# Two graph layers on degree-sorted nodes: edge j of a node as row j of its own partition, summed by VectorE, and experts that scatter their rows to the output

## The chip, the cores and the metric

The kernel runs on one core of one Trainium2 chip. The metric is the device time of one execution in microseconds, given as the median of several runs. A core has TensorE (PE, with its weight loads shown apart as PEld), VectorE (DVE), ScalarE (ACT), GpSimd (POOL) and SyncE (SP). SP, ACT and POOL issue the transfers of this kernel; an indirect transfer, which takes the address of each row from a column of indices, is issued by POOL.

## The reference

There are 6250 nodes with 256 features, and 100000 directed edges `src -> dst`, sorted by `dst`, with 64 features each. Four residual stages follow one another, each on a layer norm (LN) of x:

```python
ft = (feat @ W_fc).reshape(N, 8, 32)                 # graph layer 0
e  = leaky_relu(eh[src] + ee + et[dst])              # eh, et: ft with attn_h, attn_t; ee: edge_attr with attn_e
a  = softmax of e over the edges of each dst
x += segment_sum(ft[src] * a, dst) + bias
x += shared_mlp(LN(x)) + the best 2 of 4 experts, mixed by their gates    # FFN 0
feat_src = LN(x) @ W_src                             # graph layer 1
r  = segment_sum(feat_src[src], dst) / max(deg, 1) + LN(x)
x += relu(batch_norm(r) * gamma + beta)
x += relu(relu(LN(x) @ W1[i] + b1[i]) @ W2[i] + b2[i])   # i: the best of 32 experts of each node
```

Everything is float32.

## The kernel before

**Tiles.** The nodes lie in their given order in 49 tiles of 128 (one node on a partition, 106 in the last). The node table x stays on the chip (`x_all`, 128 x 49 x 256).

**Prep.** SP loads x, a tile at a time (L216). POOL's queue fills two tables in DRAM with zeros (L221, L226). `edge_ranges` (L150 and on) finds where the edges of each tile begin: it loads `dst` on 125 partitions (L155), and takes minima, maxima and comparisons on 128 x 49 x 50 values (among them the reduce at L185). `node_tile` (L258) normalizes a tile, transposes it (L264), multiplies by the weights (L269), and stores rows of 264 floats, features and eight `eh`, into the DRAM table `tab0`. `edge_block` (L281) loads 2048 edges' attributes through ACT's queue (L285), transposes them (L289), copies them (`evacuate`, L121 and L123), multiplies (L295) and stores eight logits an edge to `ee_d`. A maximum over all nodes and edges (L322 to L324) shifts the exponents. Two loops over further windows of edges (L424) run no round on this input.

**Graph layer 0.** A tile takes one window of 128 x 18 = 2304 consecutive edges, from the first edge of the tile on; edge p·18+k lies on partition p. An edge's partition says nothing of its destination. For each tile, in an order written out by hand under `manual_schedule`:
- `gather` (L772): 18 indirect transfers on POOL, each of 128 rows of `tab0`, into one of 8 buffers of 6 columns.
- `turn` (L779, L781): ACT makes the transposed one-hot matrix of destinations from a copy of `dst` spread over all partitions (`load_row`).
- `look_up` (L792): PE multiplies it by `et`, so each edge finds its destination's term.
- `one_hots` (L801): DVE makes the upright one-hot.
- `weights` (L812 to L821): DVE adds the logits, leaky ReLU, ACT takes the exponential.
- `spread` (L826): DVE multiplies the gathered rows by the weights, 6 columns of 256 at a time.
- `sums` (L832): PE adds the rows of each node, 18 products of one-hot and rows accumulated in PSUM (`pa`). They release the buffers to later gathers.
- `join` (L837 to L844): divides by the sum of the weights and adds to x.

FFN 0 is a generator (`ffn0`, by groups of 4 tiles, 24 steps a group); `advance` deals its steps among the parts of a tile, six a tile. The rest runs after the last tile. Its last steps store LN(x) @ W_src as rows of the DRAM table `tab1`.

**Graph layer 1.** The same windows: 18 gathers of `tab1` a tile (L358), a one-hot on DVE (L370), 18 products on PE (L414), a copy by ACT (L933).

**Rest.** Batch norm: LN again, mean and square sums by products with ones, two passes over 49 tiles (L971 to L985). `route` (L1019 and on), by groups of 4: normalize, add to x, LN, 32 router logits, the best expert, and the node's rank in it. 49 row scatters on POOL sort the LN rows by expert into `xs_d` (L1101). 80 rounds, each of 128 slots of one expert: load, transposes (L1116), two products (L1121, L1127), ReLU, store to `ys_d` by SP. Then 49 gathers of `ys_d` by each node's slot (L1135), the addition of x (L1137) and the store. Reciprocal square roots are ACT's Ln and Exp (L95, L96), each with the load of a function table.

Of the kernel before, what the change touches and what calls it, by code (L numbers as in the profile page):

```python
# [23 lines left out]
SLOPE = 0.2  # L24

K = 18
W = P * K

SPREAD = 60.0

S = 6
NG = 8

G = 4


@with_exitstack
def tile_gnn_ffn(ctx: ExitStack, tc: tile.TileContext, a: dict, out: bass.AP):
# [10 lines left out]
    ACC = D + HEADS + 1  # L49
    GROUPS = [range(g, min(g + G, NT)) for g in range(0, NT, G)]  # L50
    rows = lambda t: P if t < NT - 1 else LAST

# [4 lines left out]
    tab0 = dram.tile([N, D + HEADS], F32, name="tab0")  # L57
    tab1 = dram.tile([N, D], F32, name="tab1")
    ee_d = dram.tile([E, HEADS], F32, name="ee_d")
    xs_d = dram.tile([NS * P, D], F32, name="xs_d")  # L60
    ys_d = dram.tile([NS * P, D], F32, name="ys_d")

    dst_f = dram.tile([E], F32, name="dst_f")

    more_d = dram.tile([NT * P, ACC], F32, name="more_d")

    x = const.tile([P, NT, D], F32, name="x_all")
    et_m = const.tile([P, NT, 2 * HEADS], F32, name="et_m")
    shift_q = const.tile([P, NT, HEADS], F32, name="shift_q")
    rdeg = const.tile([P, NT], F32, name="rdeg")  # L70
    mv_all = const.tile([P, NT, 2], F32, name="mv_all")
    rs_all = const.tile([P, NT], F32, name="rs_all")

    ident = const.tile([P, P], F32, name="ident")
    make_identity(nc, ident)
    ones = const.tile([P, P], F32, name="ones")
    nc.gpsimd.memset(ones, 1.0)
    iota = const.tile([P, P], F32, name="iota")
    nc.gpsimd.iota(iota, pattern=[[1, P]], base=0, channel_multiplier=0,
                   allow_small_or_imprecise_dtypes=True)  # L80
    zeros = const.tile([P, 512], F32, name="zeros")
    nc.vector.memset(zeros, 0.0)
# [6 lines left out]
    def rsqrt(pool, out_ap, var_ap, n, eps):  # L89

        v = pool.tile([P, n], F32, name="rsq_v")
        r = pool.tile([P, n], F32, name="rsq_r")
        u = pool.tile([P, n], F32, name="rsq_u")
        nc.vector.tensor_scalar(v, var_ap, eps, None, op0=ALU.add)
        nc.scalar.activation(r, v, AF.Ln)  # L95
        nc.scalar.activation(r, r, AF.Exp, scale=-0.5)  # L96
        nc.vector.tensor_mul(u, r, r)
        nc.vector.tensor_mul(u, u, v)
        nc.vector.tensor_scalar(u, u, -0.5, 1.5, op0=ALU.mult, op1=ALU.add)
        nc.vector.tensor_mul(out_ap, r, u)  # L100

    def ln_stats(pool, tiles):

        t0, n = tiles[0], len(tiles)
        st = pool.tile([P, G, 6], F32, name="ln_st")
        for i, t in enumerate(tiles):
            nc.vector.bn_stats(st[:, i, :], x[:, t, :])
            nc.vector.bn_aggr(mv_all[:, t, :], st[:, i, :])
        rsqrt(pool, rs_all[:, t0:t0 + n], mv_all[:, t0:t0 + n, 1], n, LN_EPS)

    def ln_apply(out_ap, t):
        nc.vector.tensor_scalar(out_ap, x[:, t, :], mv_all[:, t, 0:1], rs_all[:, t:t + 1],  # L112
                                op0=ALU.subtract, op1=ALU.mult)
# [11 lines left out]
    def max_over_partitions(pool, psum, vals, n):  # L125

        p1 = psum.tile([P, P], F32, name="mx_p")
        nc.tensor.transpose(p1[:n, :], vals, ident)
        m = pool.tile([P, 1], F32, name="mx_m")
        nc.vector.tensor_reduce(m[:n], p1[:n, :], axis=AX.X, op=ALU.max)  # L130
        p2 = psum.tile([P, P], F32, name="mx_p")
        nc.tensor.transpose(p2[:, :n], m[:n].to_broadcast([n, P]), ident[:n, :n])
        r = pool.tile([P, n], F32, name="mx_r")
        nc.vector.tensor_copy(r, p2[:, :n])
        return r


    lo_b = const.tile([P, NT], F32, name="lo_b")
    start_i = const.tile([1, NT], I32, name="start_i")
    more_i = const.tile([1, NT], I32, name="more_i")  # L140
    wins_i = const.tile([1, NT], I32, name="wins_i")
    gate_i = const.tile([1, 2], I32, name="gate_i")
    t128 = const.tile([P, NT], F32, name="t128")
    nc.gpsimd.iota(t128, pattern=[[P, NT]], base=0, channel_multiplier=0,
                   allow_small_or_imprecise_dtypes=True)

    def edge_ranges(pool, psum):

        NP_ = 125
        J = E // NP_  # L150
        S = 16
        NG = J // S
        assert NP_ * NG * S == E
        d = pool.tile([P, J], I32, name="er_d", bufs=1)
        nc.scalar.dma_start(d[:NP_], dst.rearrange("(p j) -> p j", p=NP_))  # L155
        as_f = pool.tile([P, J], F32, name="er_df", bufs=1)
        nc.vector.tensor_copy(as_f[:NP_], d[:NP_])
        nc.scalar.dma_start(dst_f.rearrange("(p j) -> p j", p=NP_), as_f[:NP_])
        mn = pool.tile([P, NG], F32, name="er_mn", bufs=1)
        mx = pool.tile([P, NG], F32, name="er_mx", bufs=1)  # L160
        nc.vector.memset(mn, 1e9)
        nc.vector.memset(mx, -1.0)
        dv = d[:NP_].rearrange("p (g s) -> p g s", s=S)
        nc.vector.tensor_reduce(mn[:NP_], dv, axis=AX.X, op=ALU.min)
        nc.vector.tensor_reduce(mx[:NP_], dv, axis=AX.X, op=ALU.max)
        first = pool.tile([P, NG], F32, name="er_f", bufs=1)
        nc.gpsimd.iota(first, pattern=[[S, NG]], base=0, channel_multiplier=J,
                       allow_small_or_imprecise_dtypes=True)
        left = pool.tile([P, NG], F32, name="er_l", bufs=1)
        nc.vector.tensor_scalar(left, first, -1.0, float(E), op0=ALU.mult, op1=ALU.add)  # L170
        end = pool.tile([P, NG], F32, name="er_e", bufs=1)
        nc.vector.tensor_scalar(end, first, float(S), None, op0=ALU.add)
        tend = pool.tile([P, NT], F32, name="er_te", bufs=1)
        nc.vector.tensor_scalar(tend, t128, float(P - 1), None, op0=ALU.add)
        shp = [P, NT, NG]
        per_t = lambda v: v[:, :, None].to_broadcast(shp)
        per_g = lambda v: v[:, None, :].to_broadcast(shp)
        i1 = pool.tile(shp, F32, name="er_i1", bufs=1)
        i2 = pool.tile(shp, F32, name="er_i2", bufs=1)
        nc.vector.tensor_tensor(i1, per_g(mn), per_t(tend), op=ALU.is_le)  # L180
        nc.vector.tensor_tensor(i2, per_g(mx), per_t(t128), op=ALU.is_ge)
        nc.vector.tensor_mul(i1, i1, i2)
        res = pool.tile([P, 2 * NT], F32, name="er_res", bufs=1)
        nc.vector.tensor_mul(i2, i1, per_g(left))
        nc.vector.tensor_reduce(res[:, :NT], i2, axis=AX.X, op=ALU.max)  # L185
        nc.vector.tensor_mul(i2, i1, per_g(end))
        nc.vector.tensor_reduce(res[:, NT:], i2, axis=AX.X, op=ALU.max)
        r = max_over_partitions(pool, psum, res, 2 * NT)
        nc.vector.tensor_scalar(lo_b, r[:, :NT], -1.0, float(E), op0=ALU.mult, op1=ALU.add)
        nc.vector.tensor_scalar(start_i, lo_b[0:1], float(E - W), None, op0=ALU.min)  # L190

        span = pool.tile([1, NT], F32, name="er_sp", bufs=1)
        nc.vector.tensor_sub(span, r[0:1, NT:], lo_b[0:1])
        M = -(-E // W)
        steps = pool.tile([1, M], F32, name="er_st", bufs=1)
        nc.gpsimd.iota(steps, pattern=[[W, M]], base=W, channel_multiplier=0,
                       allow_small_or_imprecise_dtypes=True)
        cmp = pool.tile([1, NT, M], F32, name="er_c", bufs=1)
        nc.vector.tensor_tensor(cmp, steps[:, None, :].to_broadcast([1, NT, M]),
                                span[:, :, None].to_broadcast([1, NT, M]), op=ALU.is_lt)  # L200
        more = pool.tile([1, NT], F32, name="er_m", bufs=1)
        nc.vector.tensor_reduce(more, cmp, axis=AX.X, op=ALU.add)
        nc.vector.tensor_copy(more_i, more)
        nc.vector.tensor_scalar(wins_i, more, 1.0, None, op0=ALU.add)
        any_ = pool.tile([1, 1], F32, name="er_a", bufs=1)
        nc.vector.tensor_reduce(any_, more, axis=AX.X, op=ALU.max)
        nc.vector.tensor_scalar(gate_i[:, 0:1], any_, 1.0, float(NT), op0=ALU.min, op1=ALU.mult)

    with ExitStack() as st:
        pool = st.enter_context(tc.tile_pool(name="proj", bufs=3))  # L210
        one = st.enter_context(tc.tile_pool(name="proj1", bufs=1))
        psum = st.enter_context(tc.tile_pool(name="proj_ps", bufs=1, space=PSUM))

        nc.vector.memset(x[:, NT - 1, :], 0.0)
        for t in range(NT):
            nc.sync.dma_start(x[:rows(t), t, :], x_in[t * P:t * P + rows(t), :])  # L216


# [95 lines left out]
        for c in range(nb, NC_):  # L314
            edge_block(c)
# [852 lines left out]
```

## Time and profile before

| | us |
|---|---|
| median of 9 runs | 3951.92 (3931.8 to 3976.82) |
| the profiled execution | 3934.73 |
| its span | 3933.0 |
| first gather of layer 0 (L772) | 341.6 |
| first gather of layer 1 (L358) | 2149.8 |
| first scatter by expert (L1101) | 3663.1 |
| first gather of the experts' rows (L1135) | 3855.1 |
| mean granted clock of TensorE | 0.699 of full speed |

The profile is one execution, taken by the hardware profiler. A group's row gives the line in the kernel, the engine, the operation, `out<-in` and how often; behind the first bar the busy microseconds and the mean nanoseconds of one; behind the second the idle time of the engine just before such instructions and what ended most of it (`<-PE pa L832`: TensorE finishing its write of `pa` on line 832; `issue`: nothing that the profile shows). A row "by source" gives minimum, median and maximum duration and the first and last start. A row of a window gives its bounds and length, then busy time and count of PE, PEld, DVE, ACT and POOL, the granted clock, the DMA engines' busy share, and GB/s. A row of the timeline gives start, duration, and in brackets the idle time before.

### The profile page before, as it was taken

The page shows a single profiled execution, that of the slowest core. Times are in us where ns is not written, and L with a number is a line of the kernel's source. Part 1 is how long each engine was busy: PE and PEld are TensorE (multiplying, and loading weights), DVE is VectorE, ACT ScalarE, POOL GpSimd, SP SyncE. Part 2 cuts the span into 40 slices and gives each one's busy share as a digit, 9 for nine tenths or more (in the row PEclk, how much of TensorE's full clock was granted, in tenths as well). Part 3 has the DMA queues.
Part 4 walks back from the last instruction along what each step waited for, and adds up shares of the span by engine and source line. Part 5 has one row for each costly group of instructions (what it writes and reads, how often), then busy time and mean ns, then how long its engine had stood idle before and what let it go on. Part 6 is the DMA issues. An engine that isn't in the chain of part 4 may idle for free. (4 is left out here: it accounts for less than half of the span.)

```text
span 3933.0 us, 32320 instructions
## 1 busy us (share of the span) xinstructions
PE 2628.1 (67%) x9687; PEld 1800.1 (46%) x9688; DVE 1287.0 (33%) x3094; ACT 900.0 (23%) x1444; POOL 1883.1 (48%) x2087
## 2 busy tenths in 40 slices
PE   3993577866867776775786766667566666756191
PEld 3893555655555555554563333333333323445161
DVE  3551444443444443443352010010111001466153
ACT  1331333443344343343333000000000000032040
POOL 1124554544544454544421666666666666311415
PEclk9696667777777787777787566565666556765595
DMA  9354443433434343433310333333333333400255
GB/s 317 110 171 126 135 125 114 121 103 113 117 118 120 94 133 107 121 111 95 119 52 22 96 90 96 92 94 96 90 96 91 96 92 94 98 1 0 73 181 157
DMA packets 219168, 420.53 MB, mean 107 GB/s; under 512 B 70836, under 2 KB 142591, under 8 KB 212711
## 3 DMA queue, kind: packets, MB, share of 16 engines
q0 software_dynamic: 94000, 264.88, 22.7%
q1 hardware_dynamic: 100512, 113.49, 9.7%
q10 hardware_dynamic: 24472, 39.99, 3.6%
q8 instruction: 81, 1.33, 0.1%
q14 instruction: 103, 0.84, 0.1%
HBM read 361.16 MB, written 57.02 MB: 106 GB/s over the span
## 5 line engine op out<-in xcount | busy, mean ns | idle before, releaser
L772 POOL DMA_INDIRECT g<-tab,ix x882 | 837.6, 950 | 831.7 <-PE pa L832 535.6
L414 PE MATMUL pb<-g,oh 128*128 128x256 f32 x1764 | 823.1, 580 | 432.1 <-issue 310.5
L358 POOL DMA_INDIRECT g<-tab,ix x882 | 837.5, 950 | 408.8 <-issue 249.2
L414 PEld LDWEIGHTS pb<-g,oh 128*128 128x128 f32 x1764 | 408.5, 266 | 846.7 <-DMA g<-tab,ix 412.0
L832 PE MATMUL pa<-g,oh 128*128 128x265 f32 x1764 | 497.2, 438 | 16.4 <-DVE g L826 13.1
L370 DVE TENSOR_TENSOR oh<-iota_ps,df 128x2304 f32<-128x2304 f32 x49 | 125.3, 2558 | 1091.3 <-PE pb L414 586.9
L792 PE MATMUL pz<-et_m,oht 128*128 128x16 f32 x1764 | 295.0, 294 | 249.9 <-issue 212.0
L792 PEld LDWEIGHTS pz<-et_m,oht 128*128 128x128 f32 x1764 | 306.1, 250 | 293.7 <-issue 286.1
L832 PEld LDWEIGHTS pa<-g,oh 128*128 128x128 f32 x1764 | 372.8, 217 | 126.6 <-DVE g L826 27.1
L933 ACT COPY acc_all<-pb 128x256 f32<-128x256 f32 x49 | 18.2, 372 | 1237.1 <-PE pb L414 687.0
L779 ACT ACTIVATE oht<-db,nid 128x768 f32<-128x768 f32 x147 | 253.3, 1723 | 57.6 <-DMA behind<-more_d 32.4
L826 DVE TENSOR_TENSOR g<-g,pz 128x1536 f32<-128x1536 f32 x147 | 250.6, 1747 | 41.4 <-ACT g L821 37.1
L591 PE MATMUL f_tr<-ident,ln 128*128 128x128 f32 x196 | 45.3, 367 | 173.2 <-ACT ln L582 171.8
L801 DVE TENSOR_TENSOR oh<-iota,pz 128x768 f32<-128x768 f32 x147 | 136.8, 949 | 54.4 <-PE pa L832 48.1
L781 ACT ACTIVATE oht<-oht,ones 128x768 f32<-128x768 f32 x147 | 137.5, 935 | 4.8
L1124 POOL MEMSET h<- 1x128 f32 x80 | 16.3, 205 | 245.2 <-DMA tab<-row 138.5
L295 PE MATMUL e_mm<-we,attrT 128*128 128x16 f32 (+1 forms) x784 | 119.6, 297 | 19.2 <-ACT ee_s L297 10.0
L295 PEld LDWEIGHTS e_mm<-we,attrT 128*128 128x128 f32 (+1 forms) x784 | 119.4, 240 | 22.6 <-ACT ee_s L297 11.5
L1023 POOL TENSOR_TENSOR acc_all<-acc_all,beta 128x1024 f32<-128x1024 f32 (+1 forms) x13 | 29.1, 2236 | 193.5 <-DVE acc_all L1022 193.0
L837 DVE TENSOR_TENSOR pa<-pa,behind 128x265 f32<-128x265 f32 x49 | 21.5, 439 | 282.1 <-remote 234.0
L591 PEld LDWEIGHTS f_tr<-ident,ln 128*128 128x128 f32 x196 | 27.0, 177 | 189.0 <-ACT ln L582 183.6
L565 ACT ACTIVATE e<-f_mm,eb 128x512 f32<-128x512 f32 (+2 forms) x84 | 52.1, 631 | 222.3 <-remote 158.4
(257 smaller groups left out, 3047.5 us busy)
## 6 DMA issues: line engine op xcount, KB each, us to landing
db<-dst_f SPq DMA_DIRECT2D x49, 1152.0 KB
g<-tab,ix POOLq DMA_INDIRECT x1764
attr<-in_edge_attr_dram ACTq DMA_DIRECT2D x48, 512.0 KB
xs_d<-zeros POOLq DMA_DIRECT2D x10, 1024.0 KB
xs<-xs_d SPq DMA_DIRECT2D x80, 128.0 KB
ys_d<-y SPq DMA_DIRECT2D x80, 128.0 KB
more_d<-zeros POOLq DMA_DIRECT2D x1, 6492.5 KB
behind<-more_d SPq DMA_DIRECT2D x49, 132.5 KB
```

The lines of the kernel that those rows point to most:

```text
L295: nc.tensor.matmul(pe[:n, j, :], tt[:, j, :n], we2, start=True, stop=True)
L358: nc.gpsimd.indirect_dma_start(out=g[:, k, :width], out_offset=None, in_=table, in_offset=bass.IndirectOffsetOnAxis(ap=ix[:, k:k + 1], axi ...
L370: nc.vector.tensor_tensor(oh, iota_k, df[:, :, None].to_broadcast([P, K, P]), op=ALU.is_equal)
L414: nc.tensor.matmul(pa, oh[:, k, :], g[:, k, :D], start=k == 0, stop=k == K - 1)
L591: nc.tensor.transpose(pt[:, c, j, :], ln[:, j, c * P:(c + 1) * P], ident)
L772: nc.gpsimd.indirect_dma_start(out=g[:, k, :D + HEADS], out_offset=None, in_=tab0, in_offset=bass.IndirectOffsetOnAxis(ap=ix[:, j:j + 1], ...
L779: nc.scalar.activation(oht, rows_of[t].rearrange("p (q k) -> p k q", k=K)[:, k, :], AF.Abs, bias=nid[:, t:t + 1])
L781: nc.scalar.activation(oht, oht, AF.Relu, bias=ones[:, 0:1], scale=-1.0)
L792: nc.tensor.matmul(looked[t][0][:, b * S + k, :], turned[t, b][:, k, :], et_m[:, t, :], start=True, stop=True)
L801: nc.vector.tensor_tensor(oh, iota_s, df[:, b * S:(b + 1) * S, None].to_broadcast([P, S, P]), op=ALU.is_equal)
L826: nc.vector.tensor_mul(gv, gv, looked[t][1][:, b * S:(b + 1) * S, :, None].to_broadcast([P, S, HEADS, D // HEADS]))
L832: nc.tensor.matmul(pa, hots[t, b][:, k, :], blocks[t, b][:, k, :], start=b + k == 0, stop=b * S + k == K - 1)
```

## The change

`profile` (a function on the host, of the numbers of nodes and edges alone) gives each of 49 tiles of sorted nodes a number of edge slots: KT = 40, 25, 24, 23, 22, 22, 21, 21, 20, 20, 20, 19, 19, 19, 18 four times, 17 and 16 and 15 five times each, 14 and 13 four times each, 12 three times, 11, 11, 10, 10, 9. Their sum is 822. A graph that does not fit sets a gate and runs a general path (`general0`, `general1`) besides.

**Prep.** Node p·49+c lies on partition p, column c, of `rec`; x arrives in 7 transfers of 127 partitions by 7 columns (L195), its last 27 rows apart. Each partition loads the list of edges that holds its 49 nodes (960 destinations). Counts below each node come from 49 passes over it, three of seven on ACT, four on DVE; the sources of each node's edges are gathered beside it (40 numbers, 49 gathers). A node's rank by degree comes from one-hots and running sums over 43 classes by 49 columns. The projection runs on columns; `tab0` rows now have 273 floats (features with x's share of the bias, `eh`, `et`, rank). Each record (x, list, range, `et`) is scattered to its rank's row of `rec_d` (49 scatters), and `x_all` is loaded back in sorted order (8 transfers), its lists masked beyond the node's edges (a null row).

**Layer 0.** The edge attributes are gathered beside the nodes (57 transfers of up to 20 edges a node, 5 KB), transposed and multiplied in the loop of the layer; the softmax runs along the partition, with each node's own maximum. The order of tiles is 0, 48, 47, ... 1, in a ring of 50 slots. FFN steps are dealt in proportion to a tile's slots.

**Layer 1.** 822 gathers by the same lists into a ring of 72 slots; a table row holds the source's rank.

**Rest.** Batch norm uses sums that layer 1 has finished. Rows scattered to `xs_d` carry x, its scale, shift and node number; the expert loop normalizes them on ACT, adds x, and scatters 128 rows straight to the output. Reciprocal square roots are four Newton steps on DVE (15 operations).

The core of the diff, with the new functions that it calls:

```diff
@@ edge ranges and ranks
+        for c in range(0, NT, GC):
+            nc.sync.dma_start(rec[:FULL, c:c + GC, :D], xv[:, c:c + GC, :])
...
+        for g in range(0, NT, GC):
...
+            for c in range(g + 1, g + GC + 1):
+                if c <= g + 3:
+                    nc.scalar.activation(lows, win, AF.Sign, bias=half_[:, c:c + 1], scale=-1.0,
+                                         accum_out=sg[:, c:c + 1])
+                else:
+                    nc.vector.tensor_scalar(low, win, node[:, c:c + 1], 0.0, op0=ALU.is_lt, op1=ALU.add,
+                                            accum_out=cnt[:, c:c + 1])
...
+            for c in range(g, g + GC):
+                nc.gpsimd.indirect_dma_start(out=reci[:, c, LST:], out_offset=None, **by_row(srcv, reci[:, c, ST:ST + 1]))
...
+        for c in range(NT):
+            sc = nc.gpsimd.indirect_dma_start(
+                out=rec_d, out_offset=bass.IndirectOffsetOnAxis(ap=rank_i[:, c:c + 1], axis=0),
+                in_=rec[:, c, :], in_offset=None)
@@ layer 0
+        def gather_rows(t):
+            o = at_[t]
+            place[t] = ring[:, o:o + KT[t], :]
+            for j in range(KT[t]):
+                nc.gpsimd.indirect_dma_start(out=place[t][:, j, :], out_offset=None,
+                                             **by_row(tab0, xi[:, t, LST + j:LST + j + 1]))
...
-        def sums(t, b, pa):
-            for k in range(S):
-                nc.tensor.matmul(pa, hots[t, b][:, k, :], blocks[t, b][:, k, :], start=b + k == 0,
-                                 stop=b * S + k == K - 1)
+        def join(t):
+            s = psum.tile([P, D], F32, name="sum")
+            nc.vector.tensor_reduce(s, place[t][:, :, :D].rearrange("p k d -> p d k"), axis=AX.X, op=ALU.add)
+            nc.vector.tensor_add(x[:, t, :D], x[:, t, :D], s)
+            row_stats(pool, x[:, t, :D], t)
...
+            STEPS = 24 * NT / G / sum(KT) * 1.08
+            for i, t in enumerate(ORDER):
+                if i + 1 < NT:
+                    gather_rows(ORDER[i + 1])
...
+                parts = edge_parts(ORDER[i + 1]) if i + 1 < NT else iter(())
+                owed += STEPS * KT[t]
+                n = int(owed)
+                owed -= n
+                logits(t)
+                next(parts, None)
+                advance(1)
+                weights(t)
+                next(parts, None)
+                h = KT[t] // 2
+                spread(t, 0, h)
+                next(parts, None)
+                advance(1)
+                spread(t, h, KT[t])
+                for _ in parts:
+                    pass
+                if i + 2 < NT:
+                    gather_attrs(ORDER[i + 2])
+                join(t)
...
+                advance(max(n - 2, 1))
@@ layer 1
-            nc.scalar.copy(acc[:, t, :D], plain_sums(pool, psum, iota_k, df, g))
+            for j in range(k):
+                nc.gpsimd.indirect_dma_start(out=g[:, j, :], out_offset=None,
+                                             **by_row(tab1, xi[:, t, LST + j:LST + j + 1]))
...
+            nc.vector.tensor_reduce(s, g.rearrange("p k d -> p d k"), axis=AX.X, op=ALU.add)
+            nc.vector.scalar_tensor_tensor(acc[:, t, :], s, rdeg[:, t:t + 1], ln, op0=ALU.mult, op1=ALU.add)
@@ experts
-            nc.vector.tensor_scalar(y, py, 0.0, None, op0=ALU.max)
-            nc.sync.dma_start(ys_d[s * P:(s + 1) * P, :], y)
-
-        for t in range(NT):
...
-            nc.vector.tensor_add(yt[:r], yt[:r], x[:r, t, :])
-            nc.sync.dma_start(out[t * P:t * P + r, :], yt[:r])
+            nc.vector.scalar_tensor_tensor(y, py, 0.0, xs[:, :D], op0=ALU.max, op1=ALU.add)
+
+            sc = nc.gpsimd.indirect_dma_start(
+                out=out, out_offset=bass.IndirectOffsetOnAxis(ap=xs.bitcast(I32)[:, NID:], axis=0),
+                in_=y, in_offset=None, bounds_check=N - 1, oob_is_err=False)
```

## The prediction

> **What bounds the kernel now.** I read the page's head first, then its groups, the same two gather lines by source, windows of each layer, and POOL's own order of time.
>
> ```profile
> span 3933.0 us, 32320 instructions
> ...
> PE 2628.1 (67%) x9687; PEld 1800.1 (46%) x9688; DVE 1287.0 (33%) x3094; ACT 900.0 (23%) x1444; POOL 1883.1 (48%) x2087
> ...
> L772 POOL DMA_INDIRECT g<-tab,ix x882 | 837.6, 950 | 831.7 <-PE pa L832 535.6
> L414 PE MATMUL pb<-g,oh 128*128 128x256 f32 x1764 | 823.1, 580 | 432.1 <-issue 310.5
> L358 POOL DMA_INDIRECT g<-tab,ix x882 | 837.5, 950 | 408.8 <-issue 249.2
> ```
>
> No engine is full: PE has 67%. Each layer fetches 882 times 128 rows by an instruction on POOL. In layer 0 POOL then idles 831.7 us, 535.6 of it until PE's sums (L832) release a buffer; in layer 1 L414 takes 580 ns for each half of an edge column. Where the layers begin and end, and what they run at:
>
> ```profile
> L772 POOL DMA_INDIRECT g<-tab,ix x882: 947/949/1057, 341.6 to 2008.1; - x177
> ```
>
> ```profile
> L358 POOL DMA_INDIRECT g<-tab,ix x882: 947/949/964, 2149.8 to 3393.9; - x177
> ```
>
> ```profile
> core 0: us, PE busy (x) PEld busy (x) DVE busy (x) ACT busy (x) POOL busy (x), PEclk, DMA share, GB/s
> 1000.00:1500.00 500.00, 371.18 (x1479) 270.76 (x1478) 211.72 (x480) 185.14 (x251) 244.94 (x258) 0.76 0.39 114
> 2500.00:3000.00 500.00, 326.02 (x725) 167.80 (x724) 55.71 (x42) 7.82 (x21) 332.31 (x350) 0.61 0.32 93
> ```
>
> The granted clock in layer 1 is 0.61; DMA is a third busy. What a gather costs when nothing holds it, and when PE does:
>
> ```profile
> 2600.86 0.95 POOL L358 DMA_INDIRECT g<-tab,ix  x1 [0.31 <-issue]
> 2602.11 0.95 POOL L358 DMA_INDIRECT g<-tab,ix  x1 [0.30 <-issue]
> ```
>
> ```profile
> 2633.46 0.95 POOL L358 DMA_INDIRECT g<-tab,ix  x1 [9.08 <-PE pb L414]
> ```
>
> So one gather is 0.95 + 0.30 = **1.2535 us** (17 in a row around 2600), with 1057 ns at most in either layer whatever DVE does. Free of waits, 882 of them are 1106 us; layer 0 took 1808 (341.6 to 2149.8), layer 1 1249 to the first batch-norm work at 3399.
>
> **Prep (adds).** x now arrives in 7 transfers of 127 partitions with seven 1 KB pieces each (L195). How many of the 16 DMA engines such a transfer gets is the question. By the trace's packet records, x's last tile in the kernel before (106 partitions) ran two packets at once at 46 ns per KB, and the 125-partition list of destinations at most five; both counts divide the partitions. The last attribute transfer, also 106, shows it on PE's side:
>
> ```profile
> 289.99 0.26 ACTq L285 DMA_DIRECT2D attr<-in_edge_attr_dram  x1
> ```
>
> ```profile
> 301.31 0.48 PEld L289 LDWEIGHTS e_tr<-ident,attr 106*128 106x128 f32 x5 [2.96 <-DMA attr<-in_edge_attr_dram]
> ```
>
> 11.3 us for 424 KB. 127 is prime: one engine, 6223 KB x 46 ns = 286 us, so the groups land at about 46, 88, 130 ... 298 us. The other end is 16 engines: 6.4 MB at the 317 GB/s of the page's first slice, 20 us. I take the first. The small loads on ACT's queue stand behind these groups in the semaphores that they share (order of the changed kernel), the bias load behind the sixth group, and ACT's first count (L245) behind it: counting starts near 252, needs 67 us of DVE work to the ranks (49 passes over 960 elements shared by DVE and ACT, a scan and four passes over 2107 elements at 1.05 to 1.7 ns), then 49 row scatters at 1.3 us (L1101 in the kernel before: 49 in 67 us) to 387, the load back 25 us, masks and gate 10: first gather at **425**, +83.
>
> [...]
>
> **Layer 0 (removes and adds).** Gone: one-hots (136.8 us DVE), their turned copies (ACT), look-ups and sums on PE, so the 535.6 us wait on PE goes. Padded slots shrink too: each tile has as many edge slots as its largest degree may be, 822 columns for 882, plus 57 attribute gathers of up to 5 KB a row. POOL's floor is 879 x 1.2535 = 1102 us. What is late next is DVE, which now does everything between a gather and the free slot:
>
> ```profile
> L826 DVE TENSOR_TENSOR g<-g,pz x147: 1722/1749/1758, 414.6 to 2054.7; 128x1536 f32<-128x1536 f32 x147
> ```
>
> ```profile
> 326.21 0.81 DVE L322 TENSOR_REDUCE ext<-eht 128x8 f32<-128x392 f32 x1 [0.29 <-POOL eht L272]
> ```
>
> The spread stays: 1749 ns / 6 = 0.29 us a column. The new sum is a reduce along a strided axis; no row of the trace has its stride. Bounds: a contiguous reduce (L185, 2450 elements in 2.70 us) takes 1.10 ns an element, 0.28 us a column of 256; the strided L322, whose neighbour L324 starts 0.73 us after it, takes 1.86 ns for each of its 392 elements if none of that is start-up. I take 1.67 ns, some 0.07 us of start-up taken off: **0.43 us a column**, near the row that is strided too. The bound of 0.48 adds 0.8 us a tile, that of 0.28 takes off 2.5, and then POOL alone sets the pace. Small operations are 3.6 us a tile, so DVE's chain is 3.6 + 0.72 k. The FFN's steps go between: 4 us of DVE work a tile and some 3.5 us of exposed waiting (a step has about 2 us latency: 24 steps in 45 to 48 us in the tail after 2067). Steps are dealt in proportion to k, so a tile takes 3.6 + 1.17 k on DVE against POOL's 1.25 k + 1.45: 23.2 against 22.5 us at the mean k of 16.8. The two are **nearly balanced**; as the ring holds little over two tiles, I add 40 us of POOL waiting, 16 for the start (40 columns of tile 0: DVE needs 32 us while POOL has 13 of work), 24 for the last landing, spread and sum, and 48 of FFN tail. 1102 + 40 + 16 + 24 + 48 = **1230**, against 1808: -578. Attribute transposes and logits (423 pairs) move here from prep; PE, which loses 1764 sums, covers them. If that cover went, the softmax would wait, at about 1 us a tile (8.6 pairs; ACT copies eight in 1.0 us, L121). The Newton steps that replace 106 table loads (1.28 us each on ACT) add 15 small DVE operations for up to four tiles, 3 us at L812's 208 ns, within the 3.6 and the 4.
>
> **Layer 1.** 822 x 1.2535 = 1030, landing 2, last reduce 25 x 0.43 and its add 12, gate 5: **1050** against 1249, -199. DVE needs 17 x 0.43 = 7 us of each 21, so the reduce is hidden twice over, with 72 slots in the ring.
>
> **After it.** Batch norm loses two DVE operations a tile and becomes 98 matmuls twice at the 21 us of the second pass: 46 for 61. Route 166 for 193 (the table loads go). Slots 10, scatter 67 as before. Experts: 80 rounds, before at 1.49 us; POOL now has a memset (0.2) and a row scatter (1.25 to 1.37) each, ACT one more operation (0.3 + 0.36 + 0.55): 1.6 x 80 = 128, end 4. The gather, add and store after 3855 go whole (78). **421** for 534: -113.
>
> **Sum.** 425 + 1230 + 1050 + 421 = 3126 against 3933; +83 - 578 - 199 - 113 = -807. With 1.7 us outside the span, 3128 against the profiled run's 3934.73. The median of the nine runs is 1.0044 times that run: **3140**.
>
> **Rivals.**
> - **x on all engines (0.12).** Counting then starts near 55 us and prep ends near 230: 195 us less, 2945. Against it: the 106- and 125-partition packets.
> - **Layer 0 bound by DVE (0.23).** If every FFN step's 2 us is exposed (6.5 a tile), a tile is 15.7 + 13 = 28.7 us: +236, 3375. Halfway is 3260. A strided reduce twice as dear (0.86) costs as much by itself: 7.3 us a tile, about +350 at worst. For it: 1.67 ns is from a short row, and DVE is nearly balanced already. Against: before, the FFN found time between the parts in the same manner.
> - **Gathers slow down (0.05), slower than before.** Everything rests on 1701 gathers at 1.2535 us, with DVE now busy beside them most of the time, with long passes over the ring. 807/1701 = 0.47: from a cadence of 1.73 us the gain is gone, at 1.9 it is 4240. Against it: 947 to 1057 ns in layer 0, with DVE 42% busy (211.72 of 500 us). [...]
> - **It does not do what it says (0.02).** A node's degree above its tile's slots sets the gate and runs the general path besides, milliseconds. The input's largest degree is 32 and no tile of sorted nodes exceeds its slots, so only a slip would.
> - **My forecast (0.58).** 3040 to 3230.
>
> **Numbers.** Range 2920 to 3360: the first rival's time below, most of the second's above. Some 0.5% is what a measurement of this kernel can tell from no change. Faster 0.94, same 0.01, slower 0.05.
>
> **What would show it.** Prep: the transfers of x landing 41 us apart, the first row gather near 425; near 230 means the first rival. Layer 0: 879 gathers at 0.95 us, POOL idle under 150 us beyond issue, released by DVE's sum; a wait of 6 us a tile there means the second. Sum: 7.2 us at k = 17. Layer 1: about 1030 us without gaps. End: no gather after the experts, 1.6 us a round. A median gather above 1.0 us, or an issue gap above 0.4, would make it wrong everywhere.

## The result, and the profile after

The changed kernel is 1.3% slower: 4013.35 us median (20 runs, 4000.0 to 4030.51) against 3964.84 (62 runs), ratio **1.0127** (1.0109 to 1.0144; clear of 1, but a smaller change than 2%). Forecast were 3140. The profiled execution has a span of 3995.0 us, 869 more than the sum of 3126 in the prediction. One thing has to be known for all numbers below: the kernel before took about 3960 us in some series (runs made together) and about 3335 in others, once on one and the same chip, so each kernel is compared with runs of its own series, and why the two differ is a part of the finding.

The page's head and groups, after:

```profile
span 3995.0 us, 18214 instructions
...
PE 1369.2 (34%) x4590; PEld 904.5 (23%) x4590; DVE 1689.0 (42%) x3005; ACT 501.7 (13%) x1114; POOL 1962.4 (49%) x2043
...
PEclk9998655666667656656666655555555555755555
...
L853 POOL DMA_INDIRECT ring<-tab,x_all x822 | 779.8, 949 | 828.4 <-DVE sum L907 586.6
L975 POOL DMA_INDIRECT ring<-tab,x_all x822 | 850.8, 1035 | 372.5 <-issue 270.6
...
L907 DVE TENSOR_REDUCE sum<-ring 128x256 f32<-128x3840 f32 (+17 forms) x49 | 368.8, 7526 | 1.7
```

PE's work has halved (1369 us for 2628), yet POOL idles as long in layer 0 as it did before (828.4 for 831.7 us); only the name of the releaser has changed, from PE's sums to DVE's. The sum itself costs what was forecast (368.8 / 822 = 0.449 us a column, forecast 0.43). The gathers by source:

```profile
L853 POOL DMA_INDIRECT ring<-tab,x_all x822: 943/949/1080, 477.5 to 2202.5; - x165
```

```profile
L975 POOL DMA_INDIRECT ring<-tab,x_all x822: 943/949/1955, 2302.8 to 3425.6; - x165
```

And windows in each layer (length, then busy time and count of PE, PEld, DVE, ACT, POOL, clock, DMA share, GB/s):

```profile
1000.00:1500.00 500.00, 258.78 (x838) 163.41 (x839) 269.77 (x444) 70.86 (x139) 239.01 (x253) 0.63 0.34 93
2500.00:3000.00 500.00, 0.00 (x0) 0.00 (x0) 170.50 (x47) 13.78 (x23) 379.56 (x362) 0.50 0.33 95
```

In layer 0 neither DVE (270 of 500 us) nor POOL (239) nor PE (259) is full. So something between them is slow. Look at one place, ACT's copies and TensorE's work around 510 us (start, duration, in brackets the idle time before):

```profile
507.03 0.59 ACT L870 COPY attrT<-e_tr 128x512 f32<-128x512 f32 x1 [10.82 <-remote]
539.93 0.59 ACT L870 COPY attrT<-e_tr 128x512 f32<-128x512 f32 x1 [32.31 <-remote]
```

```profile
507.67 1.89 PE L874 MATMUL pz<-we,attrT 128*128 128x16 f32 x8 [9.45 <-issue]
509.40 1.09 PE L868 MATMUL e_tr<-ident,attr 128*128 128x128 f32 x4
540.57 1.89 PE L874 MATMUL pz<-we,attrT 128*128 128x16 f32 x8 [30.08 <-ACT attrT L870]
```

The second copy waits for TensorE alone, last for the transposes L868. They end at 510.49; the semaphore that tells of it is raised at 539.86 by the record, and the copy starts at 539.93. For 29 us nobody works on this chain. The completion of TensorE's work is there late, and the profile has no name for it: `remote`. I took from the instruction records every instruction of ACT, DVE and POOL that waits for TensorE, and the time from the end of what it waits for (or of its own engine's work, if later) to its start. Where that is over 1.5 us, it sums to **604 us in 82 places** in this trace. The trace of the kernel before, on which the prediction was built, holds **559 us in 112 places**.

### The profile page after: what moved, and what is told of

Read it like the earlier page. It is cut to its first block, busy times and chain, and to the rows that moved or that the text cites. A ratio compares the mean times of both kernels' runs of the same rounds, so it can differ in the third digit from the quotient of the medians.

```text
span 3995.0 us, 18214 instructions
## 1 busy us (share of the span) xinstructions
PE 1369.2 (34%) x4590; PEld 904.5 (23%) x4590; DVE 1689.0 (42%) x3005; ACT 501.7 (13%) x1114; POOL 1962.4 (49%) x2043
## 5 line engine op out<-in xcount | busy, mean ns | idle before, releaser
L853 POOL DMA_INDIRECT ring<-tab,x_all x822 | 779.8, 949 | 828.4 <-DVE sum L907 586.6
L975 POOL DMA_INDIRECT ring<-tab,x_all x822 | 850.8, 1035 | 372.5 <-issue 270.6
L980 DVE TENSOR_REDUCE sum<-ring 128x256 f32<-128x3840 f32 (+17 forms) x49 | 359.8, 7344 | 758.5 <-DMA ring<-tab,x_all 725.5
L907 DVE TENSOR_REDUCE sum<-ring 128x256 f32<-128x3840 f32 (+17 forms) x49 | 368.8, 7526 | 1.7
L874 PE MATMUL pz<-we,attrT 128*128 128x16 f32 x846 | 176.7, 342 | 454.1 <-ACT attrT L870 342.2
L874 PEld LDWEIGHTS pz<-we,attrT 128*128 128x128 f32 x846 | 166.2, 287 | 509.8 <-ACT attrT L870 375.9
L903 DVE TENSOR_TENSOR ring<-ring,pz 128x2048 f32<-128x2048 f32 (+9 forms) x98 | 231.3, 2385 | 4.2 <-DVE pz L896 2.6
L870 ACT COPY attrT<-e_tr 128x512 f32<-128x512 f32 (+3 forms) x131 | 65.8, 502 | 545.1 <-remote 337.8
L700 PE MATMUL f_mm<-lnT,ew 128*128 128x512 f32 (+2 forms) x224 | 119.5, 671 | 25.9 <-issue 13.1
L1172 POOL DMA_INDIRECT out_dram<-y,xs x80 | 78.9, 987 | 54.5 <-DVE y L1170 44.4
L868 PE MATMUL e_tr<-ident,attr 128*128 128x128 f32 x423 | 98.1, 361 | 4.6 <-DMA attr<-in_edge_attr_dram,x_all 4.6
L1168 PE MATMUL m_y<-w,h 65*128 x160 | 92.9, 683 | 10.2 <-issue 8.5
```

What stands on the lines that cost most here:

```text
L700: nc.tensor.matmul(ps[out_rows, :T], lhs, rhs, start=i == 0, stop=i == len(parts) - 1)
L853: nc.gpsimd.indirect_dma_start(out=place[t][:, j, :], out_offset=None, **by_row(tab0, xi[:, t, LST + j:LST + j + 1]))
L868: nc.tensor.transpose(pt[:, j, :], at[:, (j0 + j) * P:(j0 + j + 1) * P], ident)
L874: nc.tensor.matmul(pz[:, o:o + 2 * HEADS], tt[:, j, :], we2, start=False, stop=c + 2 * (j0 + j) + 2 == k, skip_group_check=True)
L903: nc.vector.tensor_mul(gv, gv, pz[:, j0:j1, :, None].to_broadcast([P, j1 - j0, HEADS, D // HEADS]))
L907: nc.vector.tensor_reduce(s, place[t][:, :, :D].rearrange("p k d -> p d k"), axis=AX.X, op=ALU.add)
```

## The experiments

The theory after the result: TensorE's completions arrive late, and this is the missing time (T). Rivals: one engine's load of x bounds more than was thought (R1); the FFN's steps or the order of the loop (R2). Four kernels went first. A kernel for which no ratio is given ran once.

**x on more engines.**

```diff
-            nc.sync.dma_start(rec[:FULL, c:c + GC, :D], xv[:, c:c + GC, :])
+            nc.sync.dma_start(rec[:112, c:c + GC, :D], xv[:112, c:c + GC, :])
+            nc.sync.dma_start(rec[112:FULL, c:c + GC, :D], xv[112:, c:c + GC, :])
```

> Same as the changed kernel, but each of the seven loads of x is split in two, 112 partitions and 15 partitions. In the changed kernel x's 6223 packets run on one DMA engine from 6.4 to 290.6 us. If that one engine sets the prep, x is in before 40 us, the first gather of layer 0 (477.5 us now) starts near 290 and the whole falls by about 190 us, to some 3820. Rival: the counting of edges, the source gathers and the ranks bound the prep by themselves, then the first gather moves by under 60 us. Layers 0 and 1 and the experts (1825, 1139 and 239 us) should not move either way by more than 20.

3128.59 us against 3328.05 for the kernel before, ratio 0.9404 (0.9377 to 0.9430). The first gather of layer 0 moved to 214.8 us, 230 us earlier than in the changed kernel of an equal series (445.4, below). In the changed kernel ACT's first count waits for x:

```profile
L245 ACT ACT_TABLE_LOAD x1 | 1.3, 1283 | 250.7 <-DMA rec<-in_x_dram 250.7
```

In the changed kernel x's 6223 packets of 1 KB went one after another from 6.4 to 290.6 us, some 46 ns each; at 112 and 15 partitions the 16 engines were 90% busy and more in most slices until 40 us. So the load of one packet at a time cost 230 us. But this was in the forecast (425), which took one engine for 127 partitions. The surprise is the other number, 3328: here the kernel before is 640 us faster.

**The FFN's steps after the loop**, and **2 gathers a tile**.

```diff
             def advance(n):
+                if n < 1000:
+                    return
```

> The steps of FFN 0 are all run after the last tile of layer 0 instead of between its parts; the output is the same. Theory (signals): TensorE's completions reach ACT and DVE late, after a run of gathers; the chain of each tile still crosses TensorE for the attribute transposes and logits, so the period of a tile (33 us now) falls only partly, to 27 to 30 us, and the FFN then takes 13 groups x about 46 us alone: total 4150 to 4500. Rival (FFN's work and waits between the parts are the cost): the period falls to the 22 to 23 us of POOL's gathers and the tail is added: 1130 + 600 us for the layer in place of 1825.

```diff
-            for j in range(KT[t]):
+            for j in range(2):
...
```

> Layer 0 gathers only 2 columns of each tile instead of 9 to 40 (98 in place of 822); the rest of the ring is zero, so most neighbours' rows are left out of the output. Everything else in the loop, the FFN steps, spread and sums included, stays. Theory (signals): the 25 to 30 us delays between the end of TensorE's work and its arrival at ACT and DVE come with the runs of gathers, so they go: the sum of such delays over 1.5 us in layer 0 falls from 604 us to under 100 and a tile takes 18 to 24 us in place of 33; total 3400 to 3550. Rival (the order of the loop or DVE's own work bounds): the period stays above 30 us and the total above 3900.

3876.18 and 3307.61 us, in the same series. Neither trace has a single completion over 1.5 us late, so neither could tell T from R2; the period of 33 us was gone in all four kernels. They do price the loop without delays: from the first gather to the last addition it is 1268 us as written, 1155 without the FFN (POOL's pace), some 1200 with 98 gathers in place of 822 (DVE's chain).

**A chain of hops** between TensorE and ACT, 300 beside the gathers of layer 1 and 100 after them:

```diff
...
+                ph = psum.tile([P, P], F32, name="hop_ps", bufs=1)
+                nc.tensor.transpose(ph, first if i == 0 else hop, ident)
+                nc.scalar.copy(hop, ph)
...
```

> In layer 1 a chain is added that has nothing to do with the data: TensorE transposes 128 x 128, ACT copies it back, 300 times in turn beside the gathers, and 100 times more after the last sum, without gathers (layer 1's layer norm moves from ACT to DVE). Theory (signals): beside the gathers a hop is often 10 to 30 us and the mean far above that of the 100 hops alone, which should be 1.0 to 1.5 us; 300 hops then take most of the layer's 1100 us or outlast it. Rival: a hop takes the same 1.0 to 1.5 us in both, 300 hops are done within 450 us of the start of the layer, and layer 1 is as long as before (1139) plus 100 to 150 for the second chain.

0.831 us a hop beside the gathers and 0.831 alone, the longest 0.833. In this series T falls: gathers alone delay nothing. The next series held the pair as it is.

> The changed kernel as it is, beside the kernel before in the same call. In the first call the kernel before took 3328 us in place of 3965, and in the four kernels with the changed loops no completion of TensorE reached another engine later than 1.5 us (604 us of such delays in the changed kernel's first profile). Theory: the delays belong to the place and time of the run and hit both kernels; where they are absent the changed kernel takes about 3128 + 230 = 3360 us against 3328, ratio 1.00 to 1.02, and where they are present about 4010 against 3965. Rival: the delays are the changed kernel's own doing, then without them the ratio is about 0.85 as forecast (3400 against 3965 in like conditions).

> The kernel before as it is, profiled in this call. Theory: where it takes 3328 us, the delays of TensorE's completions (559 us in its first profile) are gone from layer 0 (1808 us then, 1250 to 1400 now) and from layer 1 (1249 then, 1150 to 1200 now), and the wait on the sums L832 (535.6 us) falls below 200: what the forecast removed was in large part these delays and not the sums' work. Rival: the layers keep 1808 and 1249 us and the 640 us are gone elsewhere (prep, the last stages).

3366.59 us (10 runs) against 3335.84 (13 runs): ratio **1.0083** (1.0061 to 1.0104), where the first had 1.0127. Both kernels lose 630 to 650 us, and the ratio is nearly the same. No completion is over 1.5 us late in either trace. The loop of the changed kernel is the same in both series, and its layer 0 took 1825 us in the first and 1314.5 here, so R2 is not what cost the 511 us. POOL's gathers in the kernel before, here:

```profile
L772 POOL DMA_INDIRECT g<-tab,ix x882 | 836.6, 948 | 371.0 <-PE pa L832 172.6 <-issue 147.1 <-DMA g<-tab,ix 18.0
L358 POOL DMA_INDIRECT g<-tab,ix x882 | 835.9, 948 | 269.7 <-issue 252.9 <-DMA g<-tab,ix 13.7 <-PE pb L414 1.8
```

and in the changed one:

```profile
L853 POOL DMA_INDIRECT ring<-tab,x_all x822 | 777.9, 946 | 379.4 <-issue 238.4 <-DVE sum L907 134.0 <-DMA ring<-tab,x_all 1.2
L975 POOL DMA_INDIRECT ring<-tab,x_all x822 | 777.6, 946 | 340.1 <-issue 250.2 <-ACT ln L978 89.9
```

The wait on the sums that the forecast removed is 172.6 us and not 535.6. And ACT's copy L870, whose idle time of 545.1 us was put to `remote` for 337.8 in the first profile of the changed kernel, now waits for what it names:

```profile
L870 ACT COPY attrT<-e_tr 128x512 f32<-128x512 f32 (+3 forms) x131 | 65.7, 502 | 219.3 <-PE e_tr L868 161.6 <-DMA eb<-in_L_ffn_eb_dram 57.6
```

The kernel with the hops ran once more, later, in a series where the kernel before took 3958.92 us; it is told here for its sake.

> The same kernel as with the 300 and 100 hops before, to be read beside this call's time of the kernel before. If that is near 3330 again, a hop takes 0.83 us with and without gathers, as in the first call. If it is near 3960, the place shows the delays of the first profiles: theory (gathers delay TensorE's completions there) has the 300 hops beside gathers at a mean above 1.5 us with some of 10 to 30, and the 100 after them at 0.83; rival (the place delays them whatever runs) has both above.

It showed the delays. Beside gathers (ACT's copies):

```profile
2400.75 0.27 ACT L978 COPY hop<-hop_ps 128x128 f32<-128x128 f32 x1 [2.53 <-issue]
2403.55 0.27 ACT L978 COPY hop<-hop_ps 128x128 f32<-128x128 f32 x1 [2.54 <-remote]
```

and after the last sum, without them:

```profile
3469.91 0.27 ACT L978 COPY hop<-hop_ps 128x128 f32<-128x128 f32 x1 [0.57 <-PE hop_ps L977]
3470.73 0.27 ACT L978 COPY hop<-hop_ps 128x128 f32<-128x128 f32 x1 [0.56 <-PE hop_ps L977]
```

Of the 299 steps from hop to hop beside gathers the mean is 2.593 us, 267 are over 2 us and the longest 3.51; the first 30, in the 25 us after the first gather, still took 0.83. The 99 alone have a mean of 0.842. The added time lies between TensorE's end and ACT's start (1.3, 2.0 or 2.7 us, steps of 0.7); from ACT to TensorE it is 0.05 us throughout. VectorE does nothing from 2318 to 2376 us, and the delays begin near 2343, so its work does not set them off. So in such a series gathers do delay TensorE's completions, and in the other they do not. T holds with a condition that the kernel does not set. The chip alone is not that condition: this series and that of the pair ran on the same chip, with 3959 and 3336 us for the kernel before. All the traces divide in the same way: by a count of nearly the same kind (518 us for the kernel before and 611 for the changed one in their first profiles), the six from series at 3960 us hold 518 to 1070 us of such delays each, and the fourteen from series at 3335 us none, but for waits for a transfer.

**The expert rounds** were the second gap: 80 rounds at 2.92 us, forecast 1.6, at a clock of 0.5, while TensorE is 92% busy:

```profile
3120.00:3340.00 220.00, 201.60 (x591) 110.04 (x590) 62.74 (x148) 86.65 (x222) 88.29 (x149) 0.52 0.26 75
```

Theory: something added lets TensorE idle at full clock (1.00 in the rounds of the kernel before), the clock falls, and then TensorE itself is the bound. Five kernels ask what. First, four added transposes of the identity in each round:

> The changed kernel with four more transposes of the identity by TensorE in each of the 80 expert rounds (into a bank that nobody reads). Theory: the round of 2.9 us is the same TensorE work at a granted clock of 0.5, which falls because at full clock POOL's memset and scatter (0.2 + 0.98 + gaps, 1.9 us) leave TensorE idle for a quarter of a round; with the added work the clock stays high and a round falls to 2.2 to 2.5 us although it holds more, 40 us less in all. Rival: the clock has another cause or TensorE's work adds up: four times 0.2 to 0.4 us more, 3.7 to 4.4 us a round, 65 to 120 us more.

A miss: the 320 transposes ran between 2864 and 2969 us, before the first round, and the rounds stayed. Then without the scatter:

```diff
-            sc = nc.gpsimd.indirect_dma_start(
-                out=out, out_offset=bass.IndirectOffsetOnAxis(ap=xs.bitcast(I32)[:, NID:], axis=0),
-                in_=y, in_offset=None, bounds_check=N - 1, oob_is_err=False)
...
+                nc.sync.dma_start(out[r:r + P, :], y)
...
```

> The changed kernel with the row scatter of each expert round replaced by a plain store from SP (rows stay in the order of the slots, so the output's rows are not sorted back). Theory: POOL is then left with a memset of 0.2 us, TensorE has no wait at full clock but on ACT's layer norm, the clock stays near 1.0 and a round takes 1.5 to 1.7 us: 95 to 110 us less. Rival 1: ACT's added layer norm is what lets TensorE idle; the round stays at 2.9. Rival 2: scatters are bound by themselves; the round falls, but the clock stays at 0.5.

1.83 us a round at a clock of 1.00, 3274.98 us in all: so the clock of 0.5 comes with the scatter. How, the next pair asked.

```diff
+            idle = psum.tile([P, P], F32, name="idle")
+            for c in range(4):
+                nc.tensor.transpose(idle, xt[:, c % 2, :], ident)
```

> The earlier kernel with added transposes did not test the clock: its 320 transposes depended on nothing and ran ahead of the rounds, which stayed at 2.83 us and 0.50 (the whole was 25 to 40 us longer). Here the four added transposes of a round read the round's own transposed rows, so that they cannot leave it. Theory (the clock falls because TensorE idles at full clock while it waits for POOL): TensorE's work at full clock is then 1.6 + 0.85 us, above POOL's 1.9, the clock stays at 1.0 and a round takes 2.3 to 2.6 us, less than 2.83 although more is done. Rival: the clock stays at 0.50 and a round takes 2.83 + 4 x 0.35 = 4.2 us, 110 us more in all.

```diff
+        hs = [w.tile([HX + 1, P], F32, name=f"h{i}") for i in range(3)]
+        for h in hs:
+            nc.gpsimd.memset(h[HX:], 1.0)
...
-            h = pool.tile([HX + 1, P], F32, name="h")
-            nc.gpsimd.memset(h[HX:], 1.0)
+            h = hs[s % 3]
```

> The changed kernel with the row of ones of the hidden layer set once, in three lasting buffers, in place of a POOL memset in each round; the scatter stays. Theory: POOL then holds a scatter alone, 0.98 + 0.3 us, less than the 1.84 us that a round took without scatters, so TensorE has no more to wait for than there: clock 1.0, 1.84 to 1.95 us a round, 70 to 80 us less in all. Rival: the scatter by itself (its wait for DVE's sum, its order behind the one before) is what brings the clock down, then the round stays at 2.8.

With four transposes **more** a round falls from 2.92 to 2.37 us, the clock is 1.00, and the whole is 3317.12 us (the changed kernel: 3366.59, in the series with 3336):

```profile
3125.00:3305.00 180.00, 160.19 (x918) 105.29 (x917) 59.24 (x152) 90.51 (x228) 89.64 (x152) 1.00 0.32 92
```

So the clock is the price: work added to TensorE alone brought it back from 0.52 to 1.00. That TensorE's idling takes it down fits this, and is my reading; no run shows it by itself. But the row of ones is not what brings it down: 2.91 us a round without it at a clock of 0.50, 3364.43. My theory of POOL's memset fell. The waits of SP's queue in the changed kernel told the rest (us in total, times, longest):

```profile
SPq L1149 <- DMA out_dram<-y,xs: 189.7, 75, 8.6
```

The scatter takes its row numbers from the loaded tile `xs`. So it holds that tile, one of five, until its rows have landed; the load of the round five later stands behind it, then ACT's layer norm, then TensorE. In the kernel before, the store read `y` and `xs` was free after the transposes. Loading into the node table's 49 places, which is free by then, takes this wait away:

```diff
-            xs = pool.tile([P, NID + 1], F32, name="xs", bufs=5)
+            xs = x[:, s % NT, :NID + 1]
...
-                out=out, out_offset=bass.IndirectOffsetOnAxis(ap=xs.bitcast(I32)[:, NID:], axis=0),
+                out=out, out_offset=bass.IndirectOffsetOnAxis(ap=xi[:, s % NT, NID:NID + 1], axis=0),
```

> The changed kernel with the expert rounds' rows loaded into the 49 places of the node table, which is free by then, in place of five rotating buffers. In the changed kernel SP's load of a round waited 173 of 210 us for a transfer to the output to land, since the scatter takes its row numbers from the loaded tile and holds it; ACT's layer norm then waits for the load. Theory: those waits are what lets TensorE idle and the clock fall; without them the clock is 1.0 and a round 1.84 to 2.0 us (ACT's chain), 70 to 85 us less than 3367. Rival: the scatter brings the clock down in another way (POOL, its wait for DVE's sum): a round stays at 2.8.

> The changed kernel with the 49 places for the expert rounds' rows, once more and with an interval. In the last call its rounds took 1.87 us in place of 2.92 and the clock was 1.00 for most of them; by the expert rounds alone that is 84 us. The changed kernel stood at 1.0083 (1.0061 to 1.0104) of the kernel before where that takes 3336, and at 1.0127 where it takes 3965: so 0.983 here if the kernel before takes about 3340, 0.992 if it takes 3960. Rival (the gain of the rounds is given back by a later wait): above 1.0.

The first ran where the kernel before took 3959: 3939.42 us and 1.87 us a round. The second where it took 3333: 3244.21 us, ratio **0.9731** (0.9688 to 0.9774), 1.47 us a round:

```profile
3120.00:3230.00 110.00, 108.26 (x609) 70.80 (x607) 61.54 (x153) 82.83 (x224) 88.72 (x153) 1.00 0.45 143
```

```profile
SPq L1149 <- DMA out_dram<-y,x_all: 13.7, 15, 2.1
```

That is less than the 1.83 us a round without any scatter, so the scatter itself does not bound a round; its hold on the tile did.

**Layer 0's sum by halves**, for the 84 us that the layer took above the forecast without delays:

```diff
-            nc.vector.tensor_reduce(s, place[t][:, :, :D].rearrange("p k d -> p d k"), axis=AX.X, op=ALU.add)
...
+                nc.vector.tensor_add(g[:, :h, :D], g[:, :h, :D], g[:, k - h:k, :D])
...
```

> The changed kernel with the strided sum of layer 0 (L907) replaced by additions of halves of a tile's columns, contiguous in memory. DVE's sum costs 0.45 us a column there; additions run at 1.165 ns an element in the spread (2.385 us for 2048), 0.30 us a column. Without 724 of the 822 gathers the loop was no shorter (24.5 us a tile), and without the FFN's steps 23.6, so DVE's chain sets the pace by a little. Theory: 0.15 us x 822 less five starts of 0.15 us a tile, some 85 us off the loop (from 1268 us to about 1185), and not more, since POOL's gathers alone take 1102. Rival: TensorE's and ACT's steps between set the pace, then the loop loses under 30 us.

3325.48 us; the layer fell by some 40 us, half of what was expected. DVE did save 128 us (369.1 to 241.2), but 73 of the 822 gathers now take over 1.0 us, 74 us more in all. Of these 73, 72 overlap one of the additions, and of the other 749 also 72. A gather before one of them, the one, and DVE beside it:

```profile
564.15 0.95 POOL L853 DMA_INDIRECT ring<-tab,x_all  x1 [0.30 <-issue]
565.40 1.83 POOL L853 DMA_INDIRECT ring<-tab,x_all  x1 [0.30 <-issue]
```

```profile
563.41 1.48 DVE L903 TENSOR_TENSOR ring<-ring,pz 128x1280 f32<-128x1280 f32 x1
564.92 3.15 DVE L909 TENSOR_TENSOR ring<-ring 128x1280 f32<-128x1280 f32 x4
```

The first of the four additions ends at 566.42, and the gather 0.81 us after that. The spread L903, which reads one operand from PSUM, held none in the changed kernel without delays, nor did its reduces (longest gather of layer 0 there 997 ns).

**Together.**

> All three: x loaded as 112 and 15 partitions, ones set once, sums by halves. If the gains add up (232 + 75 + 85 from 3367): 2975 us, ratio to the kernel before 0.89. If the clock does not come back: 3050, 0.915. If the halves bring nothing: 3060.

> x loaded as 112 and 15 partitions, the 49 places, and layer 0's sums by halves. From the kernel with x, ones and halves (3068): less 75 if the rounds fall to 1.84, 2990, ratio to the kernel before 0.895; 3060 if they do not.

> x loaded as 112 and 15 partitions and the 49 places, with layer 0's sums by the strided reduce as in the changed kernel. The halves saved DVE 128 us but 73 of 822 gathers then took over 1.0 us (74 us more), and the layer fell by about 35 us net: so 3025 to 3035 here, 35 to 40 above the kernel with the halves.

> x loaded as 112 and 15 partitions, the 49 places, sums of layer 0 by halves, once more: 0.914 (0.912 to 0.917) of the kernel before where that took 3959. If this call's kernel before takes about 3340: 3068 less 75, 2990, ratio 0.895.

| kernel (x = 112 + 15) | us | kernel before | ratio |
|---|---|---|---|
| ones, halves | 3067.87 | 3344.86 | 0.9166 (0.9138 to 0.9194) |
| places, halves | 3611.27 | 3958.92 | 0.9142 (0.9120 to 0.9165) |
| places, strided sum | 3700.16 | 3958.92 | 0.9351 (0.9294 to 0.9407) |
| places, halves, again | **2970.29** | 3333.16 | **0.8904** (0.8865 to 0.8943) |

x on more engines, the 49 places and the halves beat both kernels in both kinds of series. The first missed the 2975 us of its expectation, since the ones alone do not bring the clock back: its rounds stayed at 2.8 us. Against the forecast of its expectation the last is 20 us better. The halves are worth 89 us where completions are late, more than the 35 expected; 39 gathers of layer 0 took over 1.0 us there in place of 73, which is a part of it, and the rest stays open.

## Why the prediction was wrong, step by step

The stages in us; the pair without delays is from the series with 3336 us:

| | forecast | after, first profile | after, no delays | before, first profile | before, no delays |
|---|---|---|---|---|---|
| to the first gather of layer 0 | 425 | 477.5 | 445.4 | 341.6 | 345.0 |
| layer 0 | 1230 | 1825.3 | 1314.5 | 1808.2 | 1346.1 |
| layer 1 | 1050 | 1138.7 | 1042.7 | 1249 | 1109.6 |
| the rest | 421 | 553.5 | 548.6 | 534 | 533.5 |
| span | 3126 | 3995.0 | 3351.2 | 3933.0 | 3334.2 |

- **The step that failed** is "so the 535.6 us wait on PE goes", and with it -578 for layer 0 and a good part of -199 for layer 1. The wait was for the larger part not the price of the sums. Without delays it is 172.6 us, layer 0 before is 1346 and layer 1 1110, and the change saves 32 and 67 us there. The rest was late completions, and these come, in such a series, with TensorE's work beside gathers, of which the changed kernel has plenty: attribute transposes, logits, FFN. I credited the changed kernel with rows free of delays and the kernel before with a trace full of them. Of the 869 us between the sum and the profile, 644 (3995.0 - 3351.2) are the difference between the two series: 511 in layer 0, where completions are late; 96 in layer 1, where TensorE has no work (x0 in the window) and the gathers themselves take longer (850.8 us for 777.6); 32 in prep and 5 in the rest.
- It could have been seen. The prediction's first fence has `L414 ... 432.1 <-issue 310.5`: TensorE idle, waiting for nothing that the profile shows. Without delays the row is

```profile
L414 PE MATMUL pb<-g,oh 128*128 128x256 f32 x1764 | 1006.9, 682 | 107.7 <-DMA g<-tab,ix 67.3
```

  The same in layer 0, a row that was not shown, in the first profile of before and then without delays:

```profile
L792 PE MATMUL pz<-et_m,oht 128*128 128x16 f32 x1764 | 295.0, 294 | 249.9 <-issue 212.0 <-DMA wsrc<-in_L_gnn_W_src_dram 30.6 <-ACT oht L781 5.5
```

```profile
L792 PE MATMUL pz<-et_m,oht 128*128 128x16 f32 x1764 | 234.7, 277 | 36.9 <-DMA wsrc<-in_L_gnn_W_src_dram 31.2 <-ACT oht L781 5.6
```

- **Experts, 1.6 us a round**: 2.92. I added up instructions and saw neither that the scatter keeps the loaded tile until it has landed (189.7 us of waits), nor that TensorE then runs at half its clock (0.52; 1.00 with the places). It costs 105 us of the 128 that "the rest" is above its forecast; with the places a round is 1.47.
- **Layer 0 otherwise**: 1315 without delays for 1230. The second rival was near in kind: the loop takes some 1200 us with hardly any gathers (DVE's chain and the FFN's steps), 1155 without the FFN's steps (POOL's pace) and 1262 to 1268 with both, while 1182 were forecast. POOL's idle time beyond issue is 141 us (379.4 - 238.4), under the 150 named.
- **Layer 1**: 1042.7 for 1050 without delays. With them, 212 of 822 gathers took over 1.0 us (mean 1035 ns), 73 us more in all: the third rival's sign, far below its price. 78 of the 212 overlap a reduce, and 220 of the other 610, the same share; beside the same reduces without delays the longest is 963. So the reduces are not the cause.
- **Prep**: 445.4 for 425; the first rival is out, and its price of 195 us was 230 when x was spread.
- **The sum of a column**: 0.449 us for 0.43. **It does what it says**: no general path ran.

Left open: what sets the delays off in some series; whether the issue of gathers or their transfers carry them; why single delays in layer 0 reach 29 us where a hop has 2.7 at most; what lengthens the gathers of layer 1 there.

## What to carry to other kernels

Before a wait is credited to the work that it names, look whether the waiting engine starts when that work ends, and whether its idle time says `issue` or `remote`: such time may stay when the work goes. Price both kernels by the same rows, so that what slows both drops out of the difference. A scatter held the tile that its addresses came from until it had landed (189.7 us in 75 waits of the next loads with five buffers, 13.7 us in 15 with 49 places): the buffers must cover the time from a tile's load to that landing, or a new wait takes the place of the removed one.

## What the hardware showed unexpectedly

- TensorE stayed at half clock (0.52) for 220 us while 92% busy by the profile, and at full clock (1.00) when 89% busy with four transposes more in each round. The busy share did not tell which of the two the loop ended in.
- In some series TensorE's completions reach ACT late beside 128-row gathers, by 1.3, 2.0 or 2.7 us a hop, while ACT's reach TensorE in 0.05 us.
- Additions of two SBUF operands on VectorE held gathers on POOL (the one shown 1.83 us for 0.95); in the changed kernel, without delays, reduces and products with a PSUM operand did not (longest gather 997 ns).
